# Deferred row additions and a third row load in advance in a two-layer mixture-of-experts kernel

## The chip, the cores and the metric

The kernel is one program on 1 core of a Trainium2 chip. The metric is the device time of one execution in microseconds (us). The median of several executions stands for a kernel; single executions are taken with a hardware profiler, whose page and trace the text quotes. Engines: PE multiplies matrices, DVE works on vectors, ACT evaluates activation functions, POOL issues indirect (scatter) DMAs, SP issues the other loads and stores. All arithmetic is float32.

## The reference

The input is `x`, 4 batches of 512 tokens of 256 numbers, and a context of 1024 rows per batch. Two layers follow each other; each has an attention and a routed feed-forward part:

```python
x = x + sim_attention(layernorm(x), ctx)           # layer 0
x = x + ffn0(layernorm(x))
x = x + cross_attention(layernorm(x), ctx)         # layer 1, 4 heads of 64
x = x + ffn1(layernorm(x))

def ffn0(x):        # 12 experts, top 2; 4 of the experts pass x through
    w = softmax over the two largest of (x @ gate_w.T + expert_bias)
    y[e] = silu(x @ w1[e].T) @ w2[e].T             # 256 -> 512 -> 256, 8 experts
    return sum_e w_ffn[e] * y[e] + (sum of the pass-through weights) * x

def ffn1(x):        # 8 experts, top 2
    comb = softmax over the two largest of (x @ Wg), times alpha
    h = layernorm(x) * ln_w[e] + ln_b[e]
    y[e] = gelu(h @ fc1_w[e] + fc1_b[e]) @ fc2_w[e] + fc2_b[e]   # 256 -> 1024 -> 256
    return sum_e comb[e] * y[e]
```

Only the two chosen experts of a token contribute, so the kernel computes only those.

## The kernel before, in words

**Routing by rows.** In both layers a token is routed to two experts. The kernel writes its normalized row (256 numbers, then its index of destination, then its weight: `ROW` = 258) into a table `rows` in DRAM, at a place that belongs to the expert. A place is found by counting (`pos_i`, L900). A batch has eight scatters (L920), 128 rows each: 4 groups of tokens by 2 choices. `pending` holds them as closures; `scatter_pending(n, behind)` issues n of them and orders each behind the instruction given, so that they don't hold up other work.

**Tiles.** The filled part of `rows` is cut into tiles of 128 rows of one expert. A tile goes through these steps:

- `load_rows` (SP, L1182) loads the 128 rows from an address that a register holds. It waits for all scatters.
- `tile_turn`: DVE computes `to` (L1082), the row of the result that each row goes to; PE transposes the rows (`ht`, L1091); DVE copies them to `hT` (layer 0, L1093) or scales them by the expert's layer-norm parameters (layer 1, L1097).
- `tile_up`: PE multiplies with the first weights (`hp`, L1116), ACT applies silu (L1121) or gelu (L1125) and writes `aT`.
- `tile_down`: PE multiplies with the second weights (`y`, L1141), DVE multiplies by the row's weight (`yw`, L1145), POOL sends the rows off with an indirect DMA: in layer 0 a plain store to a table `ys` (L1148), in layer 1 an addition into the result `out` (L1158).

Additions into `out` are strictly one after another, since two tiles can hold the same token: the list `written` holds the previous addition, or the batches' stores `out<-x` (L971, SP), which must have landed before.

**Loops.** `moe(L, ...)` runs the tiles of both layers with the same inner function `run(lo, hi)`. Each pass of its loop issues one row load for a tile ahead, the first half of tile i, then `tile_turn` of tile i+1, then `tile_down` of tile i−1. Weights go round in three slots (`RING`), loaded by `load_w` on SP and skipped if the slot already holds that expert. `GROUPS` makes later tiles conditional on the count of tiles; 28 tiles run in layer 0, 31 in layer 1 (besides the four early ones).

**Early tiles.** While the last batch of layer 1 is still routed, two tiles each of the experts 0 and 1 are run early from rows that earlier batches have filled (`AHEAD` = (2, 2), names `ahead0` to `ahead3`). `load_ahead` loads their rows, and the generator `tiles_ahead` yields between their parts; `layer1_attention` calls it in pieces (`PIECES`), between the steps of the routing, and `LEFT` counts the pieces that run after it. The rest is run in `moe` by `for _ in first: pass`. Their additions are ordered behind `behind`, which is `L1.spread`: the scatters of the last batch that had been issued when the call was made.

**What sets the order.** PE's order is the program's, and so is SP's in the two expert stages. On other engines a scheduler orders instructions by its own model, with explicit edges given by `after(a, b, why)`. Buffers: the pool `k4` (tag `k4`, function `t4`) has 12 buffers of one size that rows, `hT`, `yw` and layer 0's `aT` share in turn; `to` has 6.

Of the kernel before, what the change touches and what calls it, by code (L numbers as in the profile page):

```python
# [18 lines left out]
NB = 4  # L19
S = 512  # L20
# [42 lines left out]
def two_layers(ctx: ExitStack, tc: tile.TileContext, io, out):  # L63
# [604 lines left out]
    def layer1_attention(sts):  # L668

        units = []
        for b in range(NB):
            units += [(b, t, n) for t in range(NT) for n in range(NC)]
        ps, aTs = {}, {}
        routes, queries = {}, None
        kvs = mha_kvs(sts, (NB - 1,))
        done = None
        for i in range(len(units) + 4):
            if i < len(units):  # L680
                b, t, n = units[i]
                ps[i] = mha_scores(sts[b], n, t)
                unit = sts[b]
                if i + 1 < len(units) and units[i + 1][0] > 0 and units[i + 1][2] == 0:
                    bias = mha_bias(sts[units[i + 1][0]], units[i + 1][1])
                    after(bias, done, "a piece to a unit")
                done = sts[b]["unit"]
            if i < 3:
                next(kvs)
            if 0 <= i - 2 < len(units):  # L690
                b, t, n = units[i - 2]
                turns = mha_turns(sts[b], n, t, ps[i - 2][0])
                aTs[i - 2] = next(turns)
                next(turns)
            if 11 <= i < 15:
                next(kvs)
            if 0 <= i - 4 < len(units):
                b, t, n = units[i - 4]
                if n == NC - 1:
                    added = mha_out(sts[b], t)  # L700
            if 0 <= i - 3 < len(units):
                b, t, n = units[i - 3]
                mha_values(sts[b], n, t, aTs.pop(i - 3), ps.pop(i - 3)[1])
            for route in routes.values():
                next(route, None)
            if pending and (i < len(units) or i % 2 == 1):
                scatter_pending(2, unit["unit"] if i < len(units) else added)
            if i == 2:
                next(kvs)
            if queries:  # L710
                next(queries, None)
            if 0 <= i - 2 < len(units):
                next(turns)
            b = i // (2 * NT) + 1
            if b < NB and i % (2 * NT) == QUERIES:
                queries = mha_q_pieces(b, sts)
            if i == len(units) - 5:
                slots = slots_ahead()
            if i == len(units) - 3:
                tiles = tiles_ahead(slots, *load_ahead(), sts[NB - 1]["unit"])  # L720
            if i == len(units) + 2:
                next(tiles)
            b, k = divmod(i - 11, 2 * NT)
            if k == 0 and 0 <= b < NB:
                routes[b] = route_steps(L1, b)
                next(routes[b])
        scatter_pending(2, L1.normed)
        for n in PIECES:
            for _ in range(n):
                next(tiles, None)  # L730
            for route in routes.values():
                next(route, None)
            if len(L1.run) < NB:
                scatter_pending(2, L1.turned)
            if len(L1.run) == NB and L1.table is None:
                L1.table = tile_table(L1)
                scatter_pending(2, L1.tabled)
        for i in L1.biased:
            scatter_pending(2, i)
        for _ in range(LEFT):  # L740
            next(tiles)
        return slots, tiles


    def top2(lg, ne, pick):
# [33 lines left out]
    class Layer:  # L779
        def __init__(self, n, ne, nf, w, bias):  # L780
            self.n, self.ne, self.nf, self.w, self.bias = n, ne, nf, w, bias
            self.run = []
            self.state = {}
            self.done = None
            self.table = None

            self.first = (0, 0, 0) if n == 0 else (0, 0, 1)
            self.spread = []
            self.held = const.tile([P, RING], F32, tag=f"held{n}", name=f"held{n}")
            for s, e in enumerate(self.first):  # L790
                nc.gpsimd.memset(self.held[:, s : s + 1], float(e))
# [55 lines left out]
    def route_steps(L, b):  # L847
# [70 lines left out]
        def scatter(k, t):  # L918

            i = nc.gpsimd.indirect_dma_start(  # L920
                out=rows[:, :],
                out_offset=bass.IndirectOffsetOnAxis(ap=pos_i[:, k, t : t + 1], axis=0),
                in_=buf[:, k, t, :], in_offset=None,
                bounds_check=EX * REGION - 1, oob_is_err=False,
            )
            if scatters:
                tc.declare_no_dep(i.ins, group="rows", reason="no two tokens have the same row")
            for f in fills + row_loads:
                after(i, f, "the rows are filled, and those of the other layer read, before")
            tc.add_to_no_dep_group("rows", i.ins)  # L930
            scatters.append(i)
            if b == NB - 1:
                L.spread.append(i)
            return i

        pending.extend((scatter, k, t) for k in range(2) for t in range(NT))
# [190 lines left out]
                )  # L1127
        T.aTs[i] = aT

    def tile_down(T, i, name, behind=None):  # L1130

        n, nf = T.n, T.nf
        w2 = T.slot(i)[1]
        aT = T.aTs.pop(i)
        rt = T.rts.pop(i)
        to = T.tos.pop(i)
        op = mm_ps(f"y{n}_{name}")[:, 0:D]
        for f in range(nf):
            if f == nf // 2:
                yield  # L1140
            nc.tensor.matmul(  # L1141
                op, aT[:, f, :], w2[:, f * D : f * D + D], start=(f == 0), stop=(f == nf - 1)
            )
        y = t4([P, D], f"yw{n}_{name}")
        nc.vector.tensor_scalar(y, op, rt[:, D + 1 : D + 2], None, ALU.mult)  # L1145
        where = bass.IndirectOffsetOnAxis(ap=to[:, 0:1], axis=0)
        if n == 0:
            st = nc.gpsimd.indirect_dma_start(  # L1148
                out=ys[:, :], out_offset=where, in_=y, in_offset=None,
                bounds_check=2 * NB * S - 1, oob_is_err=False,  # L1150
            )
            if y_stores:
                tc.declare_no_dep(st.ins, group="ys", reason="no two tiles have the same row")
                after(st, ys_fill, "the rows are filled before")
            tc.add_to_no_dep_group("ys", st.ins)
            y_stores.append(st)
        else:
            st = nc.gpsimd.indirect_dma_start(  # L1158
                out=flat, out_offset=where, in_=y, in_offset=None,
                bounds_check=NB * S - 1, oob_is_err=False, compute_op=ALU.add,  # L1160
            )
            if behind:
                after(st, behind[-1], "the rows of the last batch first")
            for w in written:
                after(st, w, "one addition to a row at a time")
            written[:] = [st]

    def moe(L, slots, side=iter(()), first=()):
        n = L.n
        T = Tiles(L, slots)  # L1170
        tab, valid, aside, total = L.table or tile_table(L)
# [31 lines left out]
                pass  # L1203

        def run(lo, hi, at=None):
            for i in range(lo, min(lo + 2, hi)):
                load_rows(i)
            loads = [(i, part) for i in range(lo, min(lo + RING, hi)) for part in range(2)]
            for i, part in loads[:-1]:
# [2 lines left out]

            for _ in first:
                pass
            load_w(*loads[-1])
            for i in range(lo, hi + 1):
                if i < hi:
                    if i + 2 < hi:
                        load_rows(i + 2)
                    halves = tile_up(T, i, i)  # L1220
                    next(halves)
                    if i == hi - 1:
                        down(i - 1)
                    for _ in halves:
                        pass
                    if i + RING < hi:
                        load_w(i + RING, 0)
                    if i + 1 < hi:
                        turn(i + 1)
# [56 lines left out]
                masks.append((valid[:, j : j + 1], aside[:, j : j + 1]))  # L1286
        return rts, masks

    def tiles_ahead(slots, rts, masks, behind):

        T = Tiles(L1, None)
        T.slots = {0: slots[0], 1: slots[2]}
# [10 lines left out]
        for j in range(len(rts) + 1):  # L1303
# [7 lines left out]
                    turn(j + 1)  # L1311
                yield
            if j > 0:
                down = tile_down(T, j - 1, names[j - 1], L1.spread)
                next(down)
                yield
                for _ in down:
                    pass
                yield
# [42 lines left out]
                normed = sts[0]["turned"]  # L1362
        return sts

    def layer1_experts(slots, tiles):
        moe(L1, ring_slots(L1, slots), first=tiles)

    with tc.manual_schedule(engines={mybir.EngineType.PE}):
        route = layer0_attention()
        with tc.manual_schedule(engines={mybir.EngineType.SP}):  # L1370
            sts = layer0_experts(route)
        slots, tiles = layer1_attention(sts)
        with tc.manual_schedule(engines={mybir.EngineType.SP}):
            layer1_experts(slots, tiles)


def _layouts(i):
# [64 lines left out]
```

## Time and profile before

| | |
|---|---|
| median of 3 runs | 950.67 us (949.68 to 955.41) |
| the profiled execution, its own time | 946.2 us |
| its span (first to last instruction) | 944.4 us |
| mean granted PE clock | 0.989 |
| PE busy | 888.6 us |
| layer 0's tiles | about 259 to 370 us |
| end of layer 1's routing and the early tiles | up to 709 us |
| layer 1's tiles | 709 us to the end |

The page gives one execution. In its rows PE is matmul work and PEld the loading of weights into PE. A timeline row has the start, the duration, the engine, the line, the operation with its result and operands, and in brackets the idle time of the engine before it with what ended it. A waits row has the engine and line that waited, what it waited for, the sum in us, how many times, and the longest. A windows row has the stretch, its length, the busy time of PE, PEld, DVE, ACT and POOL with the number of instructions, the granted clock of PE, the busy share of the 16 DMA engines and GB/s.

### The profile page before, as it was taken

The page shows a single profiled execution, that of the slowest core. Times are in us where ns is not written, and L with a number is a line of the kernel's source. Part 1 is how long each engine was busy: PE and PEld are TensorE (multiplying, and loading weights), DVE is VectorE, ACT ScalarE, POOL GpSimd, SP SyncE. Part 2 cuts the span into 40 slices and gives each one's busy share as a digit, 9 for nine tenths or more (in the row PEclk, how much of TensorE's full clock was granted, in tenths as well). Part 3 has the DMA queues.
Part 4 walks back from the last instruction along what each step waited for, and adds up shares of the span by engine and source line. Part 5 has one row for each costly group of instructions (what it writes and reads, how often), then busy time and mean ns, then how long its engine had stood idle before and what let it go on. Part 6 is the DMA issues. An engine that isn't in the chain of part 4 may idle for free. (4 is left out here: it accounts for less than half of the span.)

```text
span 944.4 us, 15177 instructions
## 1 busy us (share of the span) xinstructions
PE 888.6 (94%) x5506; PEld 666.1 (71%) x5506; DVE 428.8 (45%) x1253; ACT 331.2 (35%) x734; POOL 226.0 (24%) x275
## 2 busy tenths in 40 slices
PE   5899999999999998999999999999989999999995
PEld 2455464645688997556675665667869999999995
DVE  5446473645623322775665776666631212121210
ACT  3322232221221111475664664565422322232221
POOL 2312014043412222000130250250741112211121
PEclk9899999999999999999999999999989999999999
DMA  9999912020178794600000122221236957777971
GB/s 311 292 254 245 285 57 86 37 98 27 54 259 260 225 324 148 223 23 1 24 1 1 46 71 110 68 69 46 74 90 215 325 152 250 213 251 231 320 236 16
DMA packets 54906, 142.05 MB, mean 150 GB/s; under 512 B 6774, under 2 KB 32813, under 8 KB 48680
## 3 DMA queue, kind: packets, MB, share of 16 engines
q1 hardware_dynamic: 39144, 102.89, 32.8%
q0 software_dynamic: 15392, 38.10, 15.6%
q8 instruction: 47, 0.77, 0.3%
q14 instruction: 35, 0.29, 0.1%
q10 hardware_dynamic: 288, 0.00, 0.0%
HBM read 131.51 MB, written 39.91 MB: 182 GB/s over the span
## 5 line engine op out<-in xcount | busy, mean ns | idle before, releaser
L1125 ACT ACTIVATE aT<-hp,w1s 128x128 f32<-128x128 f32 x248 | 67.3, 382 | 167.5 <-issue 153.2
L1116 PEld LDWEIGHTS hp<-hT,w1s 128*128 128x128 f32 x992 | 115.8, 192 | 2.3 <-DVE hT L1097 0.7
L1116 PE MATMUL hp<-hT,w1s 128*128 128x128 f32 x992 | 116.1, 275 | 0.5 <-DVE hT L1097 0.5
L1141 PE MATMUL y<-w2s,aT 128*128 128x256 f32 x496 | 112.3, 379 | 0.5 <-ACT aT L1125 0.5
L1141 PEld LDWEIGHTS y<-w2s,aT 128*128 128x128 f32 x496 | 91.8, 190 | 11.9 <-ACT aT L1125 0.7
L615 ACT ACTIVATE p<-p,s_nm 128x1024 f32<-128x1024 f32 x64 | 73.4, 1147 | 67.9 <-DVE s_nm L611 62.6
L611 DVE CUSTOM_DVE_ANT_0 p<-s,mbias 128x1024 f32<-128x1024 f32 x64 | 75.7, 1220 | 45.9 <-PE s L602 45.8
L1158 POOL DMA_INDIRECT out<-yw,to x31 | 47.8, 1541 | 178.3 <-DVE to L1082 102.8
L1145 DVE TENSOR_SCALAR yw<-y,row 128x256 f32<-128x256 f32 x59 | 28.5, 484 | 127.6 <-PE y L1141 127.6
L625 PEld LDWEIGHTS a2t<-ident,p 128*128 128x128 f32 x512 | 55.9, 141 | 41.6 <-issue 21.3
L920 POOL DMA_INDIRECT rows<-rowbuf,rt_posi x64 | 64.4, 1006 | 82.7 <-DVE rt_posi L900 26.6
L625 PE MATMUL a2t<-ident,p 128*128 128x128 f32 x512 | 71.5, 279 | 8.8 <-ACT a2T L630 4.2
L602 PE MATMUL s<-kT,q2T 64*128 64x512 f32 x256 | 66.6, 628 | 0.7 <-DVE s_nm L611 0.7
L650 PE MATMUL o<-a2T,v 128*64 128x128 f32 x1024 | 63.3, 276 | 0.1
L304 PE MATMUL s<-ctxT,q0T 128*128 128x512 f32 x128 | 61.7, 628 | 0.7 <-ACT q0T L281 0.7
L650 PEld LDWEIGHTS o<-a2T,v 128*64 128x64 f32 x1024 | 55.4, 137 | 8.5 <-issue 7.0
L630 ACT COPY a2T<-a2t 128x512 f32<-128x512 f32 x96 | 53.4, 581 | 20.9 <-PE a2t L625 20.6
L1097 DVE TENSOR_SCALAR hT<-ht,w1s 128x128 f32<-128x128 f32 x62 | 22.6, 405 | 81.8 <-PE ht L1091 79.9
L334 PE MATMUL hq<-a0T,ctxn 128*128 128x512 f32 x128 | 56.8, 596 | 0.1
L1116 PEld LDWEIGHTS hp<-hT,w0s 128*128 128x128 f32 x448 | 54.4, 192 | 2.9 <-DVE hT L1093 1.5
L1116 PE MATMUL hp<-hT,w0s 128*128 128x128 f32 x448 | 54.9, 275 | 1.0 <-DVE hT L1093 1.0
L1141 PE MATMUL y<-w0s,aT 128*128 128x256 f32 x224 | 53.1, 380 | 0.7 <-ACT aT L1121 0.7
(260 smaller groups left out, 1226.4 us busy)
## 6 DMA issues: line engine op xcount, KB each, us to landing
w1s<-in_w1p SPq DMA_DIRECT2D x34, 1030.0 KB
w2s<-in_w2p SPq DMA_DIRECT2D x34, 1024.0 KB
rows<-zeros POOLq DMA_DIRECT2D x8, 2064.0 KB
w0s<-in_w1p SPq DMA_DIRECT2D x31, 512.0 KB
w0s<-in_w2p SPq DMA_DIRECT2D x31, 512.0 KB
row<-rows SPq DMA_DIRECT2D x59, 129.0 KB
ctxT<-in_ctxT SPq DMA_DIRECT2D x4, 1024.0 KB
ctxn<-in_ctx SPq DMA_DIRECT2D x4, 1024.0 KB
```

The lines of the kernel that those rows point to most:

```text
L304: nc.tensor.matmul(sp[:, h, :], st["qT"][:, c, bass.ts(t, P)], ctxT[b][:, c, bass.ts(h, 512)], start=(c == 0), stop=(c == NC - 1),)
L334: nc.tensor.matmul(op, ctxn[b][:, j, bass.ts(c, P)], aT[:, j, :], start=(j == 0), stop=(j == NJ - 1))
L602: nc.tensor.matmul(sps[r][:, k, :], st["qT"][at, n, bass.ts(t, P)], st["kT"][at, n, bass.ts(k, 512)], start=True, stop=True,)
L611: nc.vector.tensor_tensor_reduce(p, sps[r].rearrange("p h n -> p (h n)"), st["mbias"][:, t, :], -ATT_SCALE, -ATT_SCALE * LEAST, ALU.add, A ...
L615: nc.scalar.activation(p, p, AF.Exp, bias=nm, scale=-1.0, accum_out=tot[:, r : r + 1])
L625: nc.tensor.transpose(pt[:, bass.ts(j, P)], p[:, bass.ts(4 * g + j, P)], ident)
L630: nc.scalar.copy(d, pt)
L650: nc.tensor.matmul(op[r * HD : r * HD + HD, :], st["v"][:, j, bass.ts(2 * n + r, HD)], aT[:, r, bass.ts(j, P)], start=(j == 0), stop=(j == ...
L920: i = nc.gpsimd.indirect_dma_start(out=rows[:, :], out_offset=bass.IndirectOffsetOnAxis(ap=pos_i[:, k, t : t + 1], axis=0), in_=buf[:, k, ...
L1116: nc.tensor.matmul(o, w1[:, c * ff + f * P : c * ff + f * P + P], hT[:, c, :], start=(c == 0), stop=(c == NC - 1),)
L1125: nc.scalar.activation(aT[:, f, :], hp[:, f // 4, bass.ts(f % 4, P)], AF.Gelu_apprx_tanh, bias=w1[:, at : at + 1])
L1141: nc.tensor.matmul(op, aT[:, f, :], w2[:, f * D : f * D + D], start=(f == 0), stop=(f == nf - 1))
```

## The change

Two things are changed.

1. `tile_down` in layer 1 puts the addition into a closure. For the early tiles the closures are gathered in a list `held`, and `layer1_attention` issues those gathered so far after the last scatter of the last batch; those that come later are issued in `run`, after the early tiles are finished and ahead of the last of the first weight loads. The ordering behind `L1.spread` is dropped, and the list with it. The order of the additions among themselves, and behind the stores, stays.
2. `run` issues three row loads at its start instead of two, and in the loop the row load of tile i+3 instead of i+2. This holds for both layers, since both use `run`.

```diff
@@ layer1_attention
             if i == len(units) - 3:
-                tiles = tiles_ahead(slots, *load_ahead(), sts[NB - 1]["unit"])
+                held = []
+                tiles = tiles_ahead(slots, *load_ahead(), sts[NB - 1]["unit"], held)
...
         for _ in range(LEFT):
             next(tiles)
-        return slots, tiles
+
+        for add in held:
+            add()
+        held.clear()
+        return slots, tiles, held
@@ scatter
-            if b == NB - 1:
-                L.spread.append(i)
@@ tile_down
-    def tile_down(T, i, name, behind=None):
+    def tile_down(T, i, name, hold=None):
...
-            st = nc.gpsimd.indirect_dma_start(
-                out=flat, out_offset=where, in_=y, in_offset=None,
-                bounds_check=NB * S - 1, oob_is_err=False, compute_op=ALU.add,
-            )
-            if behind:
-                after(st, behind[-1], "the rows of the last batch first")
-            for w in written:
-                after(st, w, "one addition to a row at a time")
-            written[:] = [st]
+            def add():
+                st = nc.gpsimd.indirect_dma_start(
+                    out=flat, out_offset=where, in_=y, in_offset=None,
+                    bounds_check=NB * S - 1, oob_is_err=False, compute_op=ALU.add,
+                )
+                for w in written:
+                    after(st, w, "one addition to a row at a time")
+                written[:] = [st]
+
+            if hold is None:
+                add()
+            else:
+                hold.append(add)
@@ run, in moe
-            for i in range(lo, min(lo + 2, hi)):
+            for i in range(lo, min(lo + 3, hi)):
                 load_rows(i)
...
             for _ in first:
                 pass
+            for add in held:
+                add()
+            held.clear()
             load_w(*loads[-1])
             for i in range(lo, hi + 1):
                 if i < hi:
-                    if i + 2 < hi:
-                        load_rows(i + 2)
+                    if i + 3 < hi:
+                        load_rows(i + 3)
@@ tiles_ahead
-                down = tile_down(T, j - 1, names[j - 1], L1.spread)
+                down = tile_down(T, j - 1, names[j - 1], held)
```

In the order of instructions on each engine this shows as follows. PE's and ACT's orders are the same. On POOL the eight scatters of the last batch stand in a row, and the four additions of the early tiles behind them; before, the first addition stood ahead of them, the second after the fourth scatter, and the third and fourth after the eighth. On SP the third row load stands ahead of the first weight loads, and each later row load one tile earlier. On DVE `to` of tile i+1 stands ahead of `hT` of tile i; before, `to` of tile i stood there. The store `out<-x` of the last batch was issued behind the first two additions, because it was appended to `written` after them; in the changed kernel it comes ahead of all four.

More of the change, by code (lines that the diff above doesn't have):

```diff
@@ L787, in __init__ @@
             self.first = (0, 0, 0) if n == 0 else (0, 0, 1)
-            self.spread = []
             self.held = const.tile([P, RING], F32, tag=f"held{n}", name=f"held{n}")
@@ L1157, in tile_down, with moe @@
         else:
-            st = nc.gpsimd.indirect_dma_start(
-                out=flat, out_offset=where, in_=y, in_offset=None,
-                bounds_check=NB * S - 1, oob_is_err=False, compute_op=ALU.add,
-            )
-            if behind:
-                after(st, behind[-1], "the rows of the last batch first")
-            for w in written:
-                after(st, w, "one addition to a row at a time")
-            written[:] = [st]
-    def moe(L, slots, side=iter(()), first=()):
+            def add():
[10 more added lines that the diff above has]
+                hold.append(add)
+    def moe(L, slots, side=iter(()), first=(), held=[]):
         n = L.n
@@ L1287, in load_ahead, with tiles_ahead @@
         return rts, masks
-    def tiles_ahead(slots, rts, masks, behind):
+    def tiles_ahead(slots, rts, masks, behind, held):
         T = Tiles(L1, None)
@@ L1363, in layer0_experts, with layer1_experts @@
         return sts
-    def layer1_experts(slots, tiles):
-        moe(L1, ring_slots(L1, slots), first=tiles)
+    def layer1_experts(slots, tiles, held):
+        moe(L1, ring_slots(L1, slots), first=tiles, held=held)
     with tc.manual_schedule(engines={mybir.EngineType.PE}):
@@ L1371, in two_layers @@
             sts = layer0_experts(route)
-        slots, tiles = layer1_attention(sts)
+        slots, tiles, held = layer1_attention(sts)
         with tc.manual_schedule(engines={mybir.EngineType.SP}):
-            layer1_experts(slots, tiles)
+            layer1_experts(slots, tiles, held)
 def _layouts(i):
```

## The prediction

> **What bounds the kernel now.** I read the page's part 1 and its slices first, then the TensorE (PE) timeline around the end of the second layer's routing, then the waits of PE in both expert stages, and last the POOL and SP timelines that release those waits.
>
> ```profile
> PE 888.6 (94%) x5506; PEld 666.1 (71%) x5506; DVE 428.8 (45%) x1253; ACT 331.2 (35%) x734; POOL 226.0 (24%) x275
> PE   5899999999999998999999999999989999999995
> ```
>
> PE is busy for 94% of the span, so a change that adds no matmul can gain only where PE stands still or runs slowly. One slice is 23.6 us. The 8 in the thirtieth (685 to 708) is the second layer's transition from routing to expert tiles; the first layer's tiles fill slices 12 to 16, where losses under a tenth don't show as a digit. The PE timeline has the transition:
>
> ```profile
> 696.09 3.62 PE L1141 MATMUL y_ahead<-w2s,aT_ahead 128*128 128x256 f32 x16
> 703.65 0.44 PE L1091 MATMUL ht<-ident,row 128*128 128x128 f32 x2 [3.95 <-DMA row<-rows]
> 703.93 5.31 PE L1141 MATMUL y_ahead<-w2s,aT_ahead 128*128 128x256 f32 x16
> 709.07 3.73 PE L1116 MATMUL hp<-hT,w1s 128*128 128x128 f32 x32
> ```
>
> PE waits 3.95 us for the first tile's rows. The same sixteen matmuls that took 3.62 us before the gap take 5.31 us after it: the granted clock is low there. What held the rows back is on POOL:
>
> ```profile
> 689.42 0.97 POOL L920 DMA_INDIRECT rows<-rowbuf,rt_posi  x1 [0.30 <-issue]
> 692.66 1.57 POOL L1158 DMA_INDIRECT out<-yw_ahead,to_ahead  x1 [2.27 <-DMA rows<-rowbuf,rt_posi]
> 694.54 1.03 POOL L920 DMA_INDIRECT rows<-rowbuf,rt_posi  x1 [0.31 <-issue]
> ...
> 698.44 0.97 POOL L920 DMA_INDIRECT rows<-rowbuf,rt_posi  x1 [0.30 <-issue]
> ```
>
> The addition at 692.66 stands between the fourth and the fifth scatter of the last batch. It waits 2.27 us for the scatters ahead of it and takes 1.57 us; the other four scatters wait behind it. The waits view of the first layer's tile stage (255 to 365 us), PE and then VectorE (DVE), gives the second place:
>
> ```profile
> PE ht L1091 <- DMA row<-rows: 2.2, 3, 1.1
> DVE to L1082 <- DMA row<-rows: 22.0, 19, 3.9
> ```
>
> Columns: total us, times, longest. PE rarely waits long, but DVE reaches `to` before the row in 19 of 28 tiles: rows arrive just in time.
>
> **Step 1: the additions leave the scatters.** Nothing is removed; four `out<-yw_ahead` DMAs move on POOL's queue behind the eight scatters. In the changed order the fifth to eighth scatter follow the fourth (end 690.39) at the trace's step of 1.29 us: starts 690.7, 692.0, 693.3, 694.6, last end 695.6 instead of 699.41. The first row load was issued 2.27 us after the last scatter's end (701.68), so now at 697.8; issue to transpose was 1.97 us, so `ht_0` runs at 699.8. PE ends `y_ahead` at 699.7: the gap shrinks from 3.95 to about 0.1, a gain of 3.8. I take **3.7**; the ends are 2.5 (a third row load and the batch's store contend with the first row) and 3.95.
>
> Each queue the additions are moved past: on SP the store `out<-x` of the last batch waited for the first two of them (11.7 us in SP's waits, issued at 696.58). It now waits for none, goes out at about 692.3 and, at before's 5.1 us to landing, is done at 697.4. The order turns round: the first addition now waits for that store. POOL has nothing behind the four but later additions. What waits for them is the buffer of `to` (six): tile 2's `to` (tiles counted from 0), which on DVE stands ahead of `hT_0`, needs the first addition landed; tile 3's the second, tile 4's the third, tile 5's the fourth. The first lands at 697.4 + 3.9 (quiet price: 692.66 to its landing at 696.56) = 701.3, `hT_0` is ready at 702.4, and `hp_0` wants it at 703.5. That hides the addition by 1.1 us; past that `hp_0` slides one for one.
>
> **Step 2: the clock.** If PE does not stop, `y_ahead` takes 3.62 instead of 5.31: 1.69 us. [...] By the row it is 1.7. The trace decides, since it shows the penalty; I take **1.5** and keep 0 and 1.7 as ends (a remaining gap of up to 1.4 may still throttle).
>
> **Step 3: rows three ahead, first layer.** The 25 tiles from the third to the twenty-eighth take 97.67 us (265.20 to 362.87); the clean step between two `ht` is 3.73, so 93.25 without waits: 4.4 us are lost, by tile 0.31, 0.47, 1.24, 0.07, 0.61, 0.89, and mostly under 0.3 after. A timeline row at one of the larger, and a windows row near the stage's end:
>
> ```profile
> 300.85 0.41 PE L1091 MATMUL ht<-ident,row 128*128 128x128 f32 x2 [1.07 <-DMA row<-rows]
> ```
>
> ```profile
> 345.00:350.00 5.00, 5.00 (x36) 4.64 (x35) 1.59 (x4) 0.60 (x1) 0.97 (x1) 1.00 0.97 347
> ```
>
> The windows row ends with clock, DMA share and GB/s: DMA is 97% busy there (0.97 to 0.99 at 270 to 285 too, 0.63 to 0.8 between), and a row load issued 4.4 us ahead lands after 4.4 to 5.3. The same number of loads is issued, each a tile earlier. A whole tile of 3.73 more would hide everything, but the changed DVE order takes most of it back: `to` of tile i+1 now stands ahead of `hT` of tile i. So row i+1 has to be there before `hp_i` can start, at `ht_i` + 1.95 less `to` 0.22, `hT` 0.42 and about 0.3 between engines: the deadline moves by **0.95**, not 3.73. Only the 1.24 is over it, by 0.3; with 0.5 more for longer latencies while PE asks faster, the gain is 4.4 − 0.8 = **3.6**. Ends: 0 (where DMA is saturated, earlier loads land no earlier) and 4.4.
>
> **Step 4: rows three ahead, second layer.** PE has no wait after 714 (7.24 us a tile), so the gain is 0. In steady state a row load now waits for the addition of seven tiles earlier to free its buffer, and SP's weight loads stand behind it; that addition is two tiles, 14.5 us, old. At the start a third row is issued ahead of the weight loads: 0.65 us on SP (1.31 for two), and `w1s` of tile 2 lands at about 709 against a need at 712.3: nothing. The last addition and the end of the kernel follow PE as before.
>
> **Sum.** 3.7 + 1.5 + 3.6 = 8.8 us of the profiled execution's 946.2 (span 944.4): 937.4. The median shown, 950.67, is 4.5 above that execution; on it, **941.9**.
>
> **Rivals.**
>
> *First layer gains nothing* (945.5 = 950.67 − 5.2). For: the 97% row, and `to` waiting 22.0 us in total with the row at its throat. Against: DMA is at 0.63 to 0.8 from 285 to 345, where part of the lateness lies.
>
> *The clock does not come back* (943.4 = 950.67 − 7.3). [...] Against: the gap is gone.
>
> *All of it* (938.9 to 940.6). 4.4 + 3.95 + 1.7 = 10.0, and 11.8 if the earlier half-clock stretch, which costs `hp_ahead` at 690.79 about 1.7, falls away too. For it: one idle stretch less. Against: nothing before 691 changes.
>
> *Slower: the held additions form a late chain.* Place: the four run one after another from 697.4 on, now beside the weight loads, and tile i's `to` waits for them through its six buffers; DVE waits in order, so `hT` waits too. Price: m us per addition. The fourth lands at 697.4 + 4m, and `hp_4` can start 1.5 later (`to_5`, `hT_4`), against 735.54 before. The second layer's time changes by 4m − 36.6 from m = 7.75 on (below it `hp_4`, forecast at 729.9, is not held); against the first layer's −3.6 it breaks even at m = 10.05.
>
> ```profile
> 729.25 1.54 POOL L1158 DMA_INDIRECT out<-yw,to  x1 [5.71 <-DVE to L1082]
> 739.42 1.53 POOL L1158 DMA_INDIRECT out<-yw,to  x1 [8.62 <-issue]
> ```
>
> Under weights the longest interval of two additions is these 10.17 us (others 7.2 to 8.5), all after 729. At 10.2 it is +4.2 − 3.6 = +0.6: 951.3, and 954.9 if the first layer fails as well. At 12 with that failure: 962. [...] I take the rows' 8.5 for three of them and the quiet 3.9 for the first, which lands before the weights are issued (703.98 on): 697.4 + 3.9 + 25.5 + 1.5 = 728.3, under 729.9.
>
> *It does not do what it says* (about 947 to 950.7): the last scatters wait for something other than the addition, or the third row is wholly eaten by DVE's order. POOL's line at 694.54 shows only 0.31 "issue" after the addition, which speaks against.
>
> **How the numbers follow.** Forecast 0.32, first layer nothing 0.15, no clock 0.11, all of it 0.24, slower chain 0.14, not as said 0.04. One per cent, 9.5 us, is about what a measurement of this kernel can tell from no change. Faster by more means under 941.2: all of "all of it" and a third of the forecast, 0.34. Slower by more means over 960.2: the upper two thirds of the chain case, 0.10. The rest, 0.56, is within. The range runs from 937.0 (the lowest case, 938.9, less 2 us for the runs' spread) to 952.0 (the chain at its trace price), which leaves out the worse chain cases and some of the lowest.
>
> **What would show it.** Right: eight scatters in a row on POOL, `ht_0` of the second layer at about 699.8 with a wait under 0.5, the `y_ahead` behind it at 3.62, `hp_0` at 703.5, `hp_4` near 730; in the first layer the third to the twenty-eighth `ht` within 94 us. Wrong: DVE `to` waiting for `out<-yw_ahead` after 703 and `hT` behind it; first-layer steps still at 3.9; additions over 8.9 us apart between 700 and 730.

## The result, and the profile after

The changed kernel takes 939.57 us (median of 16 runs, 936.22 to 947.15), the kernel before, in runs beside it, 950.61 (16 runs, 945.94 to 955.41). The ratio is 0.9887, 95% interval [0.9862, 0.9913]: 10.7 us less (8.3 to 13.1). A second set of runs gave 0.9877 [0.9842, 0.9912].

The profiled execution of the changed kernel took 944.76 us, the third longest of its 16; the one of before, 946.2, is among the shortest of that kernel. So their difference of 1.4 us is not the effect. The page's lines that answer to the first two of before:

```profile
PE 886.5 (94%) x5506; PEld 663.7 (70%) x5506; DVE 431.4 (46%) x1253; ACT 331.2 (35%) x734; POOL 226.0 (24%) x275
PE   5798999999999998999999999999989999999995
```

The digits are no help: the share is 94% as before, and the second and the fourth slice read 7 and 8 where before has 8 and 9. These lie in the first layer's attention, which the change doesn't touch, and they hide most of the gain in this execution: the third `ht` of layer 0 comes at 270.10 us against 265.20 before, with a granted clock of 0.87 between 20 and 60 us against 0.91. In the second profile of the same kernel it is 264.07 and 0.96. Another 1.6 us are lost between the two stages. So the stages the change touches are compared, each from its own start. Layer 1's transition comes first, in the PE timeline. There `ht_0` and `hp_0` are the transpose and the first product of layer 1's tile 0, the `ht` and the `hp` below:

```profile
694.01 3.84 PE L1118 MATMUL hp_ahead<-hT_ahead,w1s 128*128 128x128 f32 x32
697.68 3.62 PE L1143 MATMUL y_ahead<-w2s,aT_ahead 128*128 128x256 f32 x16
703.75 0.44 PE L1093 MATMUL ht<-ident,row 128*128 128x128 f32 x2 [2.45 <-DMA row<-rows]
704.03 3.62 PE L1143 MATMUL y_ahead<-w2s,aT_ahead 128*128 128x256 f32 x16
707.48 3.73 PE L1118 MATMUL hp<-hT,w1s 128*128 128x128 f32 x32
```

The wait for the first row is 2.45 us instead of 3.95, and the `y_ahead` behind it runs at 3.62, not 5.31. The granted clock agrees. Before, the windows rows behind the gap read 0.69 and 0.50 (the third number from the end); in the changed kernel it is 1.00 from 703.6 to 709.0. "Half clock" below is a stretch at 0.50, or work that takes as long as it did in one (before, `hp_ahead` 5.47 us, against 3.84 above).

```profile
704.00:706.00 2.00, 2.00 (x8) 1.70 (x8) 0.86 (x3) 0.00 (x0) 0.00 (x0) 0.69 0.69 107
706.00:708.00 2.00, 2.00 (x6) 1.55 (x6) 0.00 (x0) 0.00 (x0) 0.00 (x0) 0.50 0.02 4
```

POOL's timeline shows why the rows are earlier: the last scatters stand in a row, and the additions come behind them.

```profile
692.65 0.97 POOL L924 DMA_INDIRECT rows<-rowbuf,rt_posi  x1 [0.30 <-DVE tt_left L1031]
694.42 0.97 POOL L924 DMA_INDIRECT rows<-rowbuf,rt_posi  x1 [0.80 <-issue]
...
698.25 0.97 POOL L924 DMA_INDIRECT rows<-rowbuf,rt_posi  x1 [0.30 <-issue]
699.53 1.58 POOL L1161 DMA_INDIRECT out<-yw_ahead,to_ahead  x1 [0.30 <-issue]
703.64 1.58 POOL L1161 DMA_INDIRECT out<-yw_ahead,to_ahead  x1 [2.53 <-DMA out<-yw_ahead,to_ahead]
```

In layer 0's tile stage (waits view, 255 to 365 us, PE and then DVE; columns: total us, times, longest) PE's waits for rows are gone. What is left stands at `hp`, behind `hT`, while DVE waits longer for rows than before:

```profile
PE hp L1118 <- DVE hT L1095: 1.6, 3, 0.6
```

```profile
DVE to L1084 <- DMA row<-rows: 29.8, 21, 4.0
```

Two of PE's three waits there, 0.52 each, stand ahead of the third `ht`, as before; only one of 0.60 lies in the stage counted below. The third to the twenty-eighth `ht` take 94.24 us, before 97.67. Of these 3.4 us, 2.2 are idle time of PE (2.76 before, 0.60 after) and 1.3 are busy time (94.91 and 93.64): part of the lateness stands in PE's busy time and not in its waits.

To read layer 1's transition in profiles with different starts, its times below count from the first of the two `b<-fc2b,combT` matmuls (L965 before, L967 after; the b2 matmuls below), which stand ahead of the last early tile's `hp_ahead` in every kernel. This is what the profiles of four kernels gave, three of them profiled twice (all in us):

| kernel | layer 0, 3rd to 28th `ht` | first row's `ht` | wait there | from its `y_ahead` to `hp_0` | `hp_0` |
|---|---|---|---|---|---|
| before | 97.67 | 15.22 | 3.95 | 5.14 | 20.64 |
| third row only | 93.47 | 15.75 | 5.78 | 5.92 | 22.15 |
| third row only, again | 93.29 | 15.75 | 4.15 | 5.14 | 21.17 |
| deferred additions only | 97.37 | 12.39 | 0.91 | 3.46 | 16.12 |
| deferred additions only, again | 96.24 | 12.46 | 1.00 | 3.46 | 16.20 |
| changed kernel | 94.24 | 12.29 | 2.45 | 3.45 | 16.02 |
| changed kernel, again | 93.72 | 12.41 | 0.95 | 3.46 | 16.14 |

From `hp_0` to the end of the span it is 235.33 before, and 235.52 and 235.41 in the changed kernel: layer 1's tiles neither gain nor lose.

### The profile page after: what moved, and what is told of

The parts are those of the page before. It is cut to its first block, busy times and chain, and to the rows that moved or that the text cites. A ratio compares the mean times of both kernels' runs of the same rounds, so it can differ in the third digit from the quotient of the medians.

```text
span 943.0 us, 15236 instructions
## 1 busy us (share of the span) xinstructions
PE 886.5 (94%) x5506; PEld 663.7 (70%) x5506; DVE 431.4 (46%) x1253; ACT 331.2 (35%) x734; POOL 226.0 (24%) x275
## 4 chain that ended last, share of the span: by engine, by line
PE 36%; DMA 7%; DVE 7%; issue 5%; ACT 4%; POOL 0%; SPq 0%; POOLq 0%; ACTq 0%; DVEq 0%
PE hp L1118 9%; PE y L1143 8%; PE s L602 5%; DMA out<-yw,to 5%; PE a2t L625 4%; PE o L650 3%; ACT p L615 2%; DVE p L611 2%; PE q L586 1%; DMA row<-rows 1%; ACT a2T L630 1%; PE hp_ahead L1118 1%; PE lgT L864 1%; PE wo L665 1%; ACT L615 1%
```

## The experiments

### Each part alone

The deferred additions alone: the changed kernel with

```diff
-            for i in range(lo, min(lo + 3, hi)):
+            for i in range(lo, min(lo + 2, hi)):
...
-                    if i + 3 < hi:
-                        load_rows(i + 3)
+                    if i + 2 < hi:
+                        load_rows(i + 2)
```

> The changed kernel with the row loads two tiles ahead again in both layers: only the deferred additions remain. Theory (two independent gains: the third row is worth 3.4 us in layer 0, the deferred additions 4.6 us at layer 1's transition): layer 0's third to twenty-eighth ht take about 97.7 us again (94.2 in the changed kernel), the transition is the changed kernel's (from the first b2 matmul, L967, to hp_0 about 16.0 us), and the time is about 943, 3.4 above the changed kernel's 939.6, a ratio to before of about 0.992. Rival (the row loads do all of it, also at the transition): the time is before's, 950, with hp_0 20.6 us behind the b2 matmul. Rival (layer 0's gain was only one profile's luck): 939.6.

The third row alone: the kernel before with the opposite edit.

> The kernel before with the third row load in advance in both layers: the additions stay among the scatters. Theory: layer 0's third to twenty-eighth ht take about 94.2 us, PE still waits some 4 us for layer 1's first row, behind the first b2 matmul by 20.6 us at hp_0, and the time is about 947, a ratio of 0.9965. Rival (row loads do all of it): 939.6. Rival (the additions do all of it): 950.6.

Measured: the additions alone 944.95 against 948.86, ratio 0.9966 [0.9948, 0.9984]; the third row alone 944.27, ratio 0.9958 [0.9941, 0.9975]. The stages in the table are as the theory had them. The third row shortens layer 0 (97.67 to 93.47) and leaves the transition without a gain; the additions do the opposite. In particular the transition is 16.1 with two rows or with three, so the third row is worth nothing in layer 1. But the additions' time, 3.2 us less than before, fell short of the 4.5 of their stage. Both were run again.

> The deferred additions alone once more, since its time (3.2 less than before) fell short of its stages (5.3 less). Theory (the stages are right, the time is the spread of the runs): again about 97.5 and 16.1 us in the two stages, and a time about 5 less than before, ratio 0.9945. Rival (deferring without the third row costs something elsewhere): again 3 less, and a middle part longer than 327 as in its first profile.

> The third row alone once more. Theory: 93.5 to 94.2 us in layer 0, 20.6 to 22.2 from the first b2 matmul to hp_0, a time 3.7 less than before, ratio 0.996. Rival (the third row also helps at the transition): hp_0 under 19 us behind the b2 matmul.

Measured: 0.9944 [0.9924, 0.9965] for the additions, 5.3 us, and 0.9963 [0.9936, 0.9991] for the third row, 3.5 us. Layer 0 and the transition repeat (table). The part between layer 0's last `ht` and the first b2 matmul was 328.1 in the first profile of the additions alone, 326.8 in the second; it is 325.6 before, 327.1 and 325.5 in the two profiles of the changed kernel, and 328.3 in the first profile of the third row alone. It moves by nearly 3 us with no pattern by kernel, as does the start. The two intervals of the additions overlap (1.5 to 4.9 us and 3.3 to 7.2), and no profile shows a cost elsewhere. The clock at the gap is seen best in the third row alone, where the gap stayed:

```profile
702.96 0.69 PE L1091 MATMUL ht<-ident,row 128*128 128x128 f32 x2 [5.78 <-DMA row<-rows]
703.44 6.08 PE L1141 MATMUL y_ahead<-w2s,aT_ahead 128*128 128x256 f32 x16
```

and in its second profile

```profile
699.57 0.44 PE L1091 MATMUL ht<-ident,row 128*128 128x128 f32 x2 [4.15 <-DMA row<-rows]
699.85 5.31 PE L1141 MATMUL y_ahead<-w2s,aT_ahead 128*128 128x256 f32 x16
```

### The changed kernel once more

> The changed kernel once more, for a second profile and a time beside the runs of this round. Theory: as its first profile, 94.2 us or less for layer 0's third to twenty-eighth ht, about 16.0 us from the first b2 matmul to hp_0, no wait of PE for a tile of layer 1 after that, and a ratio to before of 0.989, of which the two stages explain about 9 us. Rival (a third source of gain outside the two stages): the middle of the kernel, from the last ht of layer 0 to the first b2 matmul, is shorter than before's 325.6 by 1 to 2 us; it was 327.1 in the first profile, which speaks against.

Measured: 937.49 against 950.64, ratio 0.9877 [0.9842, 0.9912], 11.7 us (8.4 to 15.0). The middle part, 325.46, equals before's, so no third source shows. Its transition, again on PE's timeline:

```profile
685.79 5.46 PE L1118 MATMUL hp_ahead<-hT_ahead,w1s 128*128 128x128 f32 x32
691.09 3.62 PE L1143 MATMUL y_ahead<-w2s,aT_ahead 128*128 128x256 f32 x16
695.66 0.44 PE L1093 MATMUL ht<-ident,row 128*128 128x128 f32 x2 [0.95 <-DMA row<-rows]
```

Here `hp_ahead` ran at half clock (5.46; 3.84 in the first profile), and the wait is 0.95 instead of 2.45. The row comes at 12.3 to 12.4 in both: a faster `hp_ahead` only makes PE wait longer for it. So `hp_0` stands within 0.2 us in all four profiles with deferred additions.

### What holds the first row now

All eight scatters of the last batch as soon as their places are known:

```diff
         elif b + 1 == NB:
-            scatter_pending(2)
+            scatter_pending(len(pending))
```

> The changed kernel with all eight scatters of the last batch issued as soon as their places are known, instead of two after that, two behind the tile table and two behind each addition of the bias. Theory (what is left of the gap, 2.45 us, is the pacing: the last four scatters wait for DVE's table and bias work): the last scatter starts about 9 us after the first, the wait of layer 1's first ht falls from 2.45 to under 0.5, hp_0 comes 14 us behind the first b2 matmul instead of 16.0, and the time is about 2 us less, 937.5. Rival (the pacing was needed: scatters ahead of the bias work hold up DVE or delay the table): DVE's table and bias work is later by some us, PE waits at the b2 matmuls or at ht_0 as before, and the time is that of the changed kernel or up to 3 us more.

Measured: 944.44, ratio 0.9953 [0.9936, 0.9970], about 5 to 6 us more than the changed kernel: the rival. The scatters did run in a row and the first row was no longer waited for, but DVE and with it PE stood still ahead of that (waits view, 680 to 700 us):

```profile
PE b L967 <- issue: 4.1, 1, 4.1
DVE yw_ahead L1147 <- remote: 3.7, 1, 3.7
```

`remote` stands for a release whose origin the profile does not show. DVE's `yw_ahead` began 0.15 us after the last scatter's end, and the product that it reads had been ready for over 4 us. The second b2 matmul, which takes the buffer that it frees, began 0.05 us after its end.

Half as far, four scatters first:

```diff
         elif b + 1 == NB:
-            scatter_pending(2)
+            scatter_pending(4)
```

> The changed kernel with four scatters of the last batch, instead of two, issued as soon as their places are known; two follow behind the tile table and two behind the first addition of the bias. With all eight at once DVE's yw_ahead stood still for 3.7 us. Theory (what is left of layer 1's first wait is the number of scatters that come after the bias work; a short run of scatters doesn't stop DVE): the last scatter ends 2.5 us earlier, PE's wait for the first row falls to under 0.5 and hp_0 comes 13.6 us behind the first b2 matmul instead of 16.0; the time is about 2.4 less than the changed kernel's. Rival (scatters back to back stop DVE's yw_ahead as soon as they meet it): hp_0 at 16 or more, and no gain.

Measured: the last scatter ended 5.2 us after the first b2 matmul instead of 7.7, PE's wait at the first `ht` was gone, and `hp_0` came at 14.98; `hp_ahead` took 5.47 (half clock), 1.6 more than its 3.84, which covers the difference to the 13.6 expected. The time, 938.73 (ratio 0.9878 [0.9841, 0.9914]), can't be told from the changed kernel's 937.49 in the same set.

Another way, `ht_0` behind the last `y_ahead`:

```diff
-            turn(lo)
-
             for _ in first:
                 pass
+            turn(lo)
```

> The changed kernel with the first tile's transpose ht_0 behind the last early tile's y_ahead on PE, instead of ahead of it. Theory (PE waits 2.45 us at ht_0 while y_ahead is ready): y_ahead fills the wait, ht_0 waits for nothing, hp_0 waits about 1 us for hT_0, and hp_0 comes about 14.8 us behind the first b2 matmul instead of 16.0: 1.2 us gained, 938.4. Rival (the row is not what is late, PE is held by y_ahead's operand): ht_0 and hp_0 both later by 0.9, 940.5.

Measured: 939.64, ratio 0.9899 [0.9866, 0.9932]. PE ran through both `y_ahead` without a gap, and `hp_0` waited 0.81 us for `hT_0`:

```profile
697.22 7.07 PE L1143 MATMUL y_ahead<-w2s,aT_ahead 128*128 128x256 f32 x32
704.13 0.38 PE L1093 MATMUL ht<-ident,row 128*128 128x128 f32 x2
705.32 3.93 PE L1118 MATMUL hp<-hT,w1s 128*128 128x128 f32 x32 [0.81 <-DVE hT L1099]
```

`hp_0` came at 15.94 instead of 14.8: `hp_ahead` was slow here too (5.47), so there was only about 1 us to fill, and the wait for `hT_0` gave it back. The expectation had taken 2.45 us for the usual gap; of the four profiles with deferred additions in the table three have 0.9 to 1.0.

### DVE's order in layer 0

`to` of a tile behind `hT` of the same tile, in layer 0:

```diff
             L0.turned = nc.vector.tensor_copy(hT.rearrange("p c n -> p (c n)"), pt[:, 0:D])
+            after(st, L0.turned, "the rows for the matmul first")
```

> The changed kernel with DVE's to ordered behind hT of the same tile in layer 0, so that hT of a tile no longer waits behind the next tile's row. Theory (the third row moved the deadline by about 1 us only, because to stands in front; the rest of the lateness, 0.2 to 0.95 us in the profiles so far, is rows that are later than that): the third to the twenty-eighth ht take 93.3, with no excess over 0.1 at any tile, 0.3 to 0.9 less than in the changed kernel. Rival (what is left is not the rows but PE's or the DMA's): an excess of 0.2 to 0.9 stays.

Measured: 93.29 us, no excess at any tile, 937.77 (ratio 0.9881 [0.9836, 0.9927]). That is as expected, but it decides little: one profile of the third row alone, without this edit, has 93.29 as well, and the same edit in the next kernel left 0.30 at one tile. What is left there is too small to be attributed by single profiles.

### The store behind the additions

The last batch's store made a closure and issued behind the early additions:

```diff
         for add in held:
             add()
         held.clear()
+        added = list(written)
+        st = L1.store()
+        for w in added:
+            after(st, w, "the store behind the additions")
```

> The changed kernel with the last batch's store into out issued behind the first two early additions, as in the kernel before, while these stay behind the scatters. On SP the store is ahead of the first row loads, so they wait with it. Theory (the turned order of the store and the additions is a part of the change that it can't do without): the first addition starts at the end of the scatters, the second 4 us later, the store 4 us after that, so the first row load is issued about 8.5 us after the last scatter's end instead of 2.3, PE's wait at the first ht is about 8.5 us instead of 2.45 and the y_ahead behind it runs at half clock: 6 to 8 us slower than the changed kernel. Rival (SP would have let the row loads pass, or the store's place doesn't matter): as the changed kernel.

Measured: 941.89, ratio 0.9909 [0.9876, 0.9941], 4.4 us more than the changed kernel in the same set, but not by the way that was expected. POOL's timeline:

```profile
689.59 0.97 POOL L928 DMA_INDIRECT rows<-rowbuf,rt_posi  x1 [0.30 <-issue]
690.87 1.57 POOL L1171 DMA_INDIRECT out<-yw_ahead,to_ahead  x1 [0.31 <-DVE tt_aside L1049]
692.75 1.03 POOL L928 DMA_INDIRECT rows<-rowbuf,rt_posi  x1 [0.30 <-issue]
```

Without the store ahead of them the additions went back among the scatters, since the scheduler may order POOL as it likes. The row loads passed the store on SP (issued from 699.50, the store at 704.84), and PE waited 1.74 us at the first `ht` and 1.57 more at `hp_0`, which came at 18.81. So the closure alone does not keep the additions behind the scatters. In the changed kernel it is, as far as this one run shows, the wait for the store, which can't be issued before the bias work. The case that was meant, row loads behind a store that waits for additions, was not produced and stays untried.

### Both edits together

Four scatters first, and `to` behind `hT`:

> The changed kernel with four scatters first and with to behind hT in layer 0, the two edits that each did what they should in their stage. Theory (they add up): 93.3 us for layer 0's third to twenty-eighth ht, no wait at layer 1's first ht, hp_0 13.6 to 15.0 us behind the first b2 matmul (the spread is whether hp_ahead falls into a half-clock stretch), 1.5 to 2.9 us less than the changed kernel's two stages (94.0 and 16.1 on the mean of its profiles), a ratio to before of about 0.986. Rival (the start and the middle hide differences of this size): not to be told from 0.988 by time.

Measured: 939.99, ratio 0.9916 [0.9889, 0.9944]: no better than the changed kernel. The transition took 18.64, because DVE's `yw_ahead` stood still again, for 2.2 us, and PE for 2.67 at the second b2 matmul:

```profile
687.70 0.48 DVE L1148 TENSOR_SCALAR yw_ahead<-y_ahead,row_ahead 128x256 f32<-128x256 f32 x1 [2.21 <-remote]
688.24 2.07 PE L967 MATMUL b<-fc2b,combT 8*128 8x256 f32 x4 [2.67 <-DVE yw_ahead L1148]
```

This came with the same order on POOL as in the kernel with four scatters first, which didn't stall. What stops DVE there was not found: this time a scatter's end lay 1.1 us before its start. It was seen in two of the three kernels that issue scatters earlier, and in no other profile here.

## Why the prediction was right

The forecast was 8.8 us, 941.9; measured are 10.7 (8.3 to 13.1), 939.57. From the table, layer 0 falls from 97.1 (mean of the three profiles with two rows) to 93.7 (four with three rows), 3.4; the transition from 21.3 (three) to 16.1 (four), 5.2; together 8.6. The parts' own times, each the mean of two sets, are 4.3 and 3.8, together 8.0 before rounding. The measured 10.7 and 11.7 are larger than either, but their intervals reach down to 8.3 and 8.4. The fastest execution on record is 943.64 before, 939.51 with the additions alone, 940.55 with the third row alone and 935.80 in the changed kernel: 4.1, 3.1 and 7.8 us less. They are single executions, but they point to the stages' sum. Whether 2 to 3 us more come from somewhere can't be said from these runs.

Of the signs that the prediction named, these came: eight scatters in a row, `y_ahead` at 3.62, and no `to` that waited for an early addition. These did not quite: PE's wait at `ht_0` was 0.95 and 2.45, not under 0.5; `hp_0` and `hp_4` came about 1 us later behind the b2 matmul than forecast; layer 0 took 94.24 and 93.72 against the limit of 94.

**Step 1, the gap** (forecast 3.7): the row came 15.6 us after the b2 matmul in the three profiles with additions among the scatters and 12.4 in the four without, 3.2. The mechanism is the one described; two terms were mis-sized. The fifth scatter was put at 2.27 after the first b2 matmul, right behind the fourth; it came at 2.96, because it is ordered behind DVE's addition of the bias (`L1.biased` in the code; it starts 0.77 us after that addition's end). Before, the early addition had covered this. And the time from the last scatter's end to `ht_0` was 4.53 and 4.67 instead of 4.24. The third row load, which the prediction took for the lower end of this step, is not the reason. With two row loads, in the additions alone, it was 4.60 and 4.71 as well:

```profile
696.78 0.98 POOL L924 DMA_INDIRECT rows<-rowbuf,rt_posi  x1 [0.30 <-issue]
699.98 1.11 SPq L1188 DMA_DIRECT2D row<-rows  x2
702.36 0.44 PE L1093 MATMUL ht<-ident,row 128*128 128x128 f32 x2 [0.91 <-DMA row<-rows]
```

With three row loads and the additions among the scatters (the third row alone) it was 4.42 and 4.30. So most of it came with the deferred additions; by what way is not shown. A wait of 0.9 to 2.45 us is left, not 0.1.

**Step 2, the clock** (forecast 1.5): the stretch from `y_ahead` to `hp_0` fell from 5.14 or 5.92 to 3.46, 1.7 to 2.5, 1.9 on the mean. The row of before was a good guide: behind the gaps of 3.95, 4.15 and 5.78 us `y_ahead` took 5.31, 5.31 and 6.08, and behind those of 0.91 to 2.45 it took 3.62. The 1.5 was the author's estimate, a little under the row's 1.69 (5.31 less 3.62); no run shows it by itself, and the runs showed 1.9 in its place. Step 1 came 0.5 short and step 2 gave 0.4 more, so that their sum meets the forecast's 5.2 to a tenth is luck.

**Step 3, layer 0** (forecast 3.6): 3.4. As described the remaining wait moved from `ht` to `hp`, behind a DVE that now waits for the next tile's row (29.8 us in all, 22.0 before). What lead is left was enough; how much DVE's order gave back was not measured by itself, since the run with `to` behind `hT` decides nothing. In the working, the terms of the deadline as they stand give 1.01 and not 0.95, which changes nothing. The DMA share between 285 and 345 us was misread: its rows run from 0.63 to 0.97, not to 0.8, so the reason given against the rival that layer 0 gains nothing was weaker than it read. That rival is refuted by all four profiles with three rows.

**Step 4, layer 1** (forecast 0): 235.41 and 235.52 from `hp_0` to the end against 235.33, and the additions alone, with two rows, have 235.41 and 235.44. The two profiles of the third row alone, 235.14 and 236.01, lie on both sides.

**The rival on the slower side**, the chain of held additions: its price came, its cost didn't. The first four started at 699.53, 703.64, 708.88 and 717.39. Further on came longer intervals, first one of 9.36 us that ended with the landing of the addition before, and later some as long as the break-even:

```profile
724.58 1.53 POOL L1161 DMA_INDIRECT out<-yw,to  x1 [5.66 <-DVE hT L1099]
733.94 1.53 POOL L1161 DMA_INDIRECT out<-yw,to  x1 [7.82 <-DMA out<-yw,to]
...
775.44 1.54 POOL L1161 DMA_INDIRECT out<-yw,to  x1 [5.22 <-DVE hT L1099]
785.58 1.54 POOL L1161 DMA_INDIRECT out<-yw,to  x1 [8.60 <-DVE yw L1147]
796.22 1.54 POOL L1161 DMA_INDIRECT out<-yw,to  x1 [9.10 <-issue]
```

The last two are 10.14 and 10.64 us; before has 10.17 and, not in the prediction's count, 10.19, and the second profile of the changed kernel has 9.37 at most. But these intervals belong to tiles 0 to 9, and those of the first four additions, 4.1, 5.2 and 8.5, are within what the forecast took. DVE's `to` waited for additions in six places (in none in the second profile), and PE for none of them (waits views of the first profile, 700 and 720 us to 944):

```profile
DVE to L1084 <- DMA out<-yw,to: 6.6, 6, 1.8
```

```profile
PE y L1143 <- ACT aT L1127: 0.5, 1, 0.5
```

**All of it** was a rival at 938.9 to 940.6; the measured time lies there. By the stages it is nevertheless the forecast's own case. The gap did not go in full. The earlier half-clock stretch at `hp_ahead` was absent in only one of the four profiles with deferred additions, and there PE waited for the row that much longer instead.

## What to carry to other kernels

An addition or store that nobody waits for still costs if it stands, with a wait of its own, in the queue of transfers that somebody does wait for (here the first row came 3.2 us later for it); move it behind them, and see what in the order then holds it there. An earlier load is worth the shift of its last deadline over all consumers: here, by the forecast's count, a small index computation ahead of the main one took 2.8 of 3.7 us (not measured by itself), and the rest was enough because the lateness came in small pieces, one of 1.24 us and the others under 1. And when a gain of 1% is looked for in one profile per kernel, read the stages from their own starts: the start and the middle of this kernel moved by 3 to 6 us between profiles, as much as either part of the change.

## What the runs showed of the hardware that was not expected

Half clock also set in behind almost no idle time. `hp_ahead` stands right behind the two b2 matmuls, which have 8 rows of operands, with only 0.18 to 0.50 us of waiting between these two; it took 5.46 or 5.47 us instead of 3.84 in nine of the thirteen profiles (before, the granted clock is 0.50 from 691.5 to 694.5). PE also ran slowly behind a wait of only 2.67 us: the second b2 matmul of the kernel with both edits took 2.07 instead of 1.13. Why is open in both cases. A vector instruction whose input had long been computed stood still for 3.7 us while POOL was in a row of eight scatters, and in another kernel for 2.2; what it waited for is open.
